# A graph transformer layer on one core: the search for edge windows by columns, the order of early loads, and the engine that computes two factors

## The chip, the cores and the metric

The kernel runs on one core of a Trainium2 chip (trn2). The metric is the device time of one execution in microseconds (us); given is the median of three runs. In the profile the engines are called PE (TensorE, matrix products; PEld is its weight load), DVE (VectorE), ACT (ScalarE), POOL (GpSimd) and SP (SyncE, which only issues transfers). Each engine takes its instructions in the order in which they were built, and waits at an instruction until the semaphores that it names are reached.

## The reference, cut to what matters

3125 nodes with 256 features, 53,125 edges sorted by their destination, float32. The layer normalizes x, adds a graph convolution and a linear attention with its own feed-forward part, and then a mixture of 16 experts.

```python
xn = _layernorm(x)
# graph part: weighted sum over the edges that end in a node, then a product
msgs = edge_weight[:, None] * xn[src]
agg = segment_sum(msgs, dst, 3125)
gnn = agg @ W.T + b
# mixer: linear attention over all nodes, 8 heads
Q, K, v = elu(xn @ Wq) + 1, elu(xn @ Wk) + 1, xn @ Wv / L
KV = einsum('nshd,nshv->nhdv', K, v)
...
msg = layernorm(attention @ Wm, g1, b1)
h = relu(concatenate([xn, msg]) @ W1) @ W2
mix = xn + layernorm(h, g2, b2)
x = x + gnn + mix
# experts: the best 2 of 16 for each node
x = x + moe(_layernorm(x))
```

## The kernel before

The nodes are laid out as 25 tiles (t) of 125 rows; a tile is 128 partitions by 256 features of `x_all`. All is in one program of one core; a scheduler of the framework orders instructions on each engine, and `tc.issue_after(instruction)` tells it behind which instruction some work is to stand.

The first stage goes over the 25 tiles. `moments` takes mean and variance of a batch of tiles (BATCHES gives the batches: tiles 0-1, 2-4, 5-9, 10-14, 15-19, 20-24) with bn_stats and bn_aggr, and the reciprocal root with a chain of small DVE instructions (`rsqrt`, L81 to L88). It also makes two factors, `by` (L347) and `less` (L348, L349). `normed(t)` makes the normalized tile `xn` on DVE (L361), transposes it on PE (L371), copies it to `xnT` on ACT (L372), and then rewrites the tile of `x_all` as x * by + less on ACT (L374) and adds the constant row `cb` on POOL (L375): this is x + xn plus two biases, the sum to which later parts are added. `projected(t)` multiplies the tile by the weights of the graph part, of the keys and of the values (L383, L385), makes `k_sb` from the keys (ACT L387 and L389, DVE L391), `v_sb` from the values with a column of ones (L393, L394), and `y_all` (L395), which is also stored in DRAM as `y_d` (L396). `summed` adds keys by values to `pkv` (L402), one tile behind.

Beside this stage runs `windows`, a generator whose pieces are put between the tiles (`pieces`; `normed` takes the next piece at tiles 1, 5, 6, 11, 12 and 13, and what is left is taken ahead of tile 16). It finds where the edges of each group of five nodes begin. There are 625 groups, kept as 125 partitions by GC = 5 columns. The destinations lie as 125 rows of 425 (`dst_sb`). The heads of the rows are compared with each group's first node (`cmp_h`, L214 to L219); POOL fetches that row for each group with an indirect DMA, one for each column (`rows`, L223); all columns are compared at once (`cmp_r`, L229, 125x2125), summed (L231), turned into a start (L232 to L235, `start_i`) and stored (L236); then POOL fetches a window of 128 edges for each group (`win`, L240, five indirect DMAs). From the windows come keys and weights (L246 to L285), which `adjacency` turns into blocks of the adjacency matrix: two wide DVE instructions (`one` L295, `wone` L300), 12 matmuls (L315), an ACT copy (L318), a store to DRAM (L319). There are 157 of these in a list `todo`; one is made per tile from tile 16 on, the others between the pieces of the mixer groups. A loop behind the stage (L440) would mend windows that are too short; its count, `loops`, is computed.

Then come seven mixer groups (L597: tiles, adjacencies and early messages of each group), the last messages with the gating, and the experts.

Loads: SP issues x of tiles 0-1, then `dst_sb`, then x of tiles 2-4 and 5-9, then Wq, Wm, W1, W2 and the constant rows behind `out` (L176), then the stores `y_d` as they come. ACT issues the three projection weights (`wcat`) and x of tiles 10-24 ahead of its first compute instruction. POOL issues small constants. A transfer's issue can wait for an older transfer that used the same semaphore.

Of the kernel before, what the change touches and what calls it, by code (L numbers as in the profile page):

```python
# [8 lines left out]
F32 = mybir.dt.float32  # L9
BF16 = mybir.dt.bfloat16  # L10
I32 = mybir.dt.int32
AF = mybir.ActivationFunctionType
ALU = mybir.AluOpType
AX = mybir.AxisListType
# [3 lines left out]
N = 3125  # L18
C = 256
E = 53125  # L20
P = 128
V = 125
# [4 lines left out]
F = 512  # L27
LANES = 128
# [12 lines left out]
EJ = E // V  # L41
GN = 5
NG = N // GN
GC = NG // V
WIN = 128
# [4 lines left out]
BATCHES = ((0, 2), (2, 5), (5, 10), (10, 15), (15, 20), (20, 25))  # L50
# [4 lines left out]
def tile_gps_layer(ctx: ExitStack, tc: tile.TileContext, a: dict, out: bass.AP):  # L55
    nc = tc.nc
# [12 lines left out]
    def row_bcast(src, n, name, pool=const):  # L69
        t = pool.tile([P, n], F32, name=name)  # L70
        nc.gpsimd.dma_start(t, bass.AP(tensor=src.tensor, offset=src.offset, ap=[[0, P], [1, n]]))
        return t
# [67 lines left out]
    first = ExitStack()  # L140
    w_first = first.enter_context(tc.tile_pool(name="w_first", bufs=1))
    dst_sb = w_mix.tile([V, EJ], I32, name="dst_sb")
    b2 = row_bcast(a["b2"], C, "b2", w_mix)
    gnn_b = row_bcast(a["gnn_b"], C, "gnn_b", w_mix)

    def load_x(queue, t0, t1):
        queue.dma_start(x_all[:, t0:t1, :], a["x"][:, t0:t1, :])

    wcat = w_mix.tile([128, 2, 3 * C], F32, name="wcat")
    load_x(nc.sync, *BATCHES[0])  # L150
    nc.sync.dma_start(dst_sb, a["dst"].rearrange("(p j) -> p j", p=V))
    for i, name in enumerate(("gnn_WT", "Wk", "Wv")):
        nc.scalar.dma_start(wcat[:, :, i * C : (i + 1) * C], a[name].rearrange("(k p) o -> p k o", p=128))

    for batch in BATCHES[1:3]:
        load_x(nc.sync, *batch)
    for batch in BATCHES[3:]:
        load_x(nc.scalar, *batch)
    wq = w_mix.tile([128, 2, C], F32, name="wq")
    nc.sync.dma_start(wq, a["Wq"].rearrange("(k p) o -> p k o", p=128))  # L160
    wm = w_mix.tile([128, 2, C], F32, name="wm")
    nc.sync.dma_start(wm, a["Wm"].rearrange("(k p) o -> p k o", p=128))
    w1 = w_mix.tile([128, 4, F], F32, name="w1")
    nc.sync.dma_start(w1, a["W1"].rearrange("(k p) o -> p k o", p=128))
    w2 = w_mix.tile([128, 4, C], F32, name="w2")
    nc.sync.dma_start(w2, a["W2"].rearrange("(k p) o -> p k o", p=128))
    g1 = const.tile([128, 2], F32, name="g1")
    nc.gpsimd.dma_start(g1, a["g1"])
    b1 = const.tile([128, 2], F32, name="b1")
# [2 lines left out]
    gate_b = row_bcast(a["gate_b"], NE, "gate_b")  # L172
    gate_w = const.tile([128, 2, NE], F32, name="gate_w")
    nc.gpsimd.dma_start(gate_w, a["gate_w"].rearrange("(k p) e -> p k e", p=128))

    nc.sync.dma_start(out[N:, :].rearrange("(p r) (k c) -> p (r k) c", r=2, k=2),  # L176
                      ones[:, None, :].to_broadcast([LANES, 4, P]))
    cb = w_mix.tile([P, C], F32, name="cb")
    nc.gpsimd.tensor_tensor(cb, b2, gnn_b, op=ALU.add)

# [18 lines left out]
    def windows():  # L199
# [13 lines left out]
        shape = [V, GC, V]  # L213
# [9 lines left out]
            nc.gpsimd.indirect_dma_start(out=rows[:, i, :], out_offset=None, in_=dst_v,  # L223
                                         in_offset=bass.IndirectOffsetOnAxis(ap=row_i[:, i : i + 1], axis=0))
        yield
        cmp_r = prep.tile([V, GC, EJ], BF16, name="cmp_r")
        start_f = prep.tile([V, GC], F32, name="start_f")
        shape = [V, GC, EJ]
        nc.vector.tensor_tensor(cmp_r, rows, thr[:, :, None].to_broadcast(shape), op=ALU.is_lt)  # L229
        yield  # L230
        nc.vector.tensor_reduce(start_f, cmp_r, AX.X, ALU.add)  # L231
        nc.vector.scalar_tensor_tensor(start_f, row_f, float(EJ), start_f, op0=ALU.mult, op1=ALU.add)  # L232
        nc.vector.tensor_scalar(start_f, start_f, float(E - WIN), None, op0=ALU.min)
        start_i = prep.tile([V, GC], I32, name="start_i")
        nc.vector.tensor_copy(start_i, start_f)  # L235
        nc.sync.dma_start(first_d.rearrange("(i r) o -> r (i o)", r=V), start_i)  # L236

        win = prep.tile([V, GC, WIN, 3], I32, name="win")
        for i in range(GC):
            nc.gpsimd.indirect_dma_start(out=win[:, i, :, :].rearrange("p e w -> p (e w)"), out_offset=None,  # L240
                                         in_=a["edges"][:, :],
                                         in_offset=bass.IndirectOffsetOnAxis(ap=start_i[:, i : i + 1], axis=0))
        yield
        shape = [V, GC, WIN]
        src_f = prep.tile(shape, F32, name="src_f")
# [92 lines left out]
    mv = w_mix.tile([P, NT, 2], F32, name="mv")  # L338
    by = w_mix.tile([P, NT], F32, name="by")
    less = w_mix.tile([P, NT], F32, name="less")  # L340
    ready = {}

    def moments(t0, t1):
        for i in range(t0, t1):
            stats(mv[:, i, :], x_all[:, i, :])
        ready[t0] = rsqrt(mv[:, t0:t1, 1], t1 - t0)
        nc.gpsimd.tensor_scalar(by[:, t0:t1], ready[t0], 1.0, None, op0=ALU.add)  # L347
        nc.gpsimd.tensor_tensor(less[:, t0:t1], mv[:, t0:t1, 0], ready[t0], op=ALU.mult)  # L348
        nc.gpsimd.tensor_scalar(less[:, t0:t1], less[:, t0:t1], -1.0, None, op0=ALU.mult)  # L349

    pieces = windows()
    with tc.issue_after(next(pieces).ins):
# [1 line left out]
    def normed(t):  # L354

        nonlocal rstd, r0
        for t0, t1 in BATCHES:
            if t == t0:
                rstd, r0 = ready.pop(t0), t0
        xn = work.tile([P, C], F32, name="xn", bufs=4)  # L360
        ins = nc.vector.tensor_scalar(xn, x_all[:, t, :], mv[:, t, 0:1], rstd[:, t - r0 : t - r0 + 1],  # L361
                                      op0=ALU.subtract, op1=ALU.mult)
        with tc.issue_after(ins.ins):
            if t in (1, 5, 6, 11, 12, 13):
                next(pieces, None)
            for b in range(len(BATCHES) - 1):
                if t == BATCHES[b][0] + 1:
                    moments(*BATCHES[b + 1])
        ptr = a_ps.tile([128, 2, P], F32, name="tok", bufs=3)
        for k in range(2):  # L370
            nc.tensor.transpose(ptr[:, k, :], xn[:, k * 128 : (k + 1) * 128], ident)  # L371
        nc.scalar.copy(xnT[:, :, t * P : (t + 1) * P], ptr)  # L372

        nc.scalar.activation(x_all[:, t, :], x_all[:, t, :], AF.Identity, scale=by[:, t : t + 1], bias=less[:, t : t + 1])  # L374
        nc.gpsimd.tensor_tensor(x_all[:, t, :], x_all[:, t, :], cb, op=ALU.add)  # L375

    def projected(t):

        cols = slice(t * P, (t + 1) * P)
        pyk = a_ps.tile([P, 2 * C], F32, name="big")  # L380
        pv = a_ps.tile([P, C], F32, name="tok", bufs=3)
        for k in range(2):
            nc.tensor.matmul(pyk, lhsT=xnT[:, k, cols], rhs=wcat[:, k, : 2 * C], start=(k == 0), stop=(k == 1))  # L383
        for k in range(2):
            last = nc.tensor.matmul(pv, lhsT=xnT[:, k, cols], rhs=wcat[:, k, 2 * C :], start=(k == 0), stop=(k == 1))  # L385
        ek = work.tile([P, C], F32, name="ek", bufs=2)
        nc.scalar.activation(ek, pyk[:, C:], AF.Exp)  # L387
        k_sb = work.tile([P, C], F32, name="k_sb")
        nc.scalar.activation(k_sb, pyk[:, C:], AF.Relu)  # L389

        nc.vector.scalar_tensor_tensor(k_sb, ek, 1.0, k_sb, op0=ALU.min, op1=ALU.add)  # L391
        v_sb = work.tile([P, 2, 129], F32, name="v_sb")
        nc.vector.memset(v_sb[:, :, 128:129], 1.0)  # L393
        nc.scalar.activation(v_sb[:, :, :128], pv.rearrange("p (c v) -> p c v", c=2), AF.Copy, scale=1.0 / N)  # L394
        nc.scalar.copy(y_all[:, t, :], pyk[:, :C])  # L395
        nc.sync.dma_start(y_d[t * P : (t + 1) * P, :], y_all[:, t, :])  # L396
        return last, k_sb, v_sb

    def summed(t, k_sb, v_sb):
# [6 lines left out]
    kept = None  # L406
    normed(0)
    for t in range(NT):
        if t == 16:
            for _ in pieces:  # L410
                pass
            prep_pool.close()
            nbr = first.enter_context(tc.tile_pool(name="nbr", bufs=3))
            half = ExitStack()
            hot = half.enter_context(tc.tile_pool(name="hot", bufs=3))
        if t + 1 < NT:
            normed(t + 1)
        if t >= 16:
            adjacencies(1)
        last, *taken_on = projected(t)  # L420

        if kept is not None:
            with tc.issue_after(last.ins):
                summed(t - 1, *kept)
        kept = taken_on
# [168 lines left out]
            nc.vector.scalar_tensor_tensor(xt, hw[:, i, :], rstd[:, i : i + 1], xt, op0=ALU.mult, op1=ALU.add)  # L594

    t = 0
    for nt, n_adj, n_early in ((4, 16, 0), (4, 22, 6), (4, 22, 7), (4, 22, 7), (3, 22, 6), (3, 22, 7), (3, 22, 2)):  # L597

        pieces = 3 * nt + 6
        i = 0  # L600
        for p, _ in enumerate(mixer(t, nt)):
            while i < n_adj and i * pieces < (p + 1) * n_adj:
                adjacencies(1)
                i += 1
                if i * n_early // n_adj > (i - 1) * n_early // n_adj:
                    messages(*early.pop(0))
        adjacencies(n_adj - i)
        t += nt
# [554 lines left out]
```

## Time and profile before

| what | value |
|---|---|
| median of 3 runs | 1083.58 us |
| lowest, highest | 1080.57, 1085.25 us |
| the profiled execution | 1079.18 us |
| its span | 1077.5 us |
| mean granted clock of PE in it | 0.991 |
| ACT busy share, POOL busy share | 25%, 20% |
| PE busy in the stretch 20 to 40 us, 40 to 60 us | 14.52, 13.15 us |
| DVE in these | 14.33, 11.58 us |
| share of the 16 DMA engines in 0 to 20, 20 to 40, 40 to 60 us | 0.92, 0.57, 0.39 |

An engine's busy share is the time in which it has an instruction under way. The page's slices cut the span into 40 equal parts, with a digit for the tenths of each that were busy; the row PEclk gives the clock that PE was granted. A wait is named by the instruction that stood waiting, and by what released it.

### The profile page before, as it was taken

What the parts mean: (1) busy time and instruction counts of PE and PEld (TensorE: products, weight loads), DVE (VectorE), ACT (ScalarE), POOL (GpSimd) and SP (SyncE); (2) the same over time, 40 slices, a digit from 0 to 9 for tenths busy, and PEclk for the clock granted to TensorE, in tenths of its full rate; (3) what the DMA queues carried; (4) which work ended last, traced back from release to release, by engine and by line L of the source; (5) the groups of instructions that cost most, each with busy time, mean ns of one, the idle gap of its engine ahead of it and who ended that gap; (6) DMA issues with size and microseconds to landing.
All of it is one profiled execution on the core that took longest, in us unless ns stands there. A gap on an engine that the chain in (4) does not pass through costs nothing.

```text
span 1077.5 us, 16415 instructions
## 1 busy us (share of the span) xinstructions
PE 1022.2 (95%) x6074; PEld 824.2 (76%) x6074; DVE 612.2 (57%) x1741; ACT 266.9 (25%) x582; POOL 215.0 (20%) x211
## 2 busy tenths in 40 slices
PE   4699989999999999999999999989999999999995
PEld 2467666778678787878878888878788888888884
DVE  5697695859579497976981135565942222222221
ACT  2456442333323333232320000103111111111110
POOL 6642000000000000000000001012454544454432
PEclk9899999999999999999999999999999999999998
DMA  9402241324234243444434454574665767576762
GB/s 279 99 25 85 103 170 66 118 88 166 100 131 163 89 144 141 157 157 156 167 101 156 158 174 139 179 260 154 186 174 162 239 201 233 168 230 183 225 194 27
DMA packets 70754, 165.66 MB, mean 154 GB/s; under 512 B 10966, under 2 KB 30318, under 8 KB 66698
## 3 DMA queue, kind: packets, MB, share of 16 engines
q1 hardware_dynamic: 50264, 133.14, 35.8%
q0 software_dynamic: 15904, 25.43, 10.8%
q10 hardware_dynamic: 4498, 5.95, 1.6%
q8 instruction: 50, 0.82, 0.3%
q14 instruction: 38, 0.31, 0.1%
HBM read 106.06 MB, written 58.40 MB: 153 GB/s over the span
## 4 chain that ended last, share of the span: by engine, by line
PE 64%; DVE 19%; DMA 3%; issue 1%; POOL 0%; ACT 0%; DVEq 0%; POOLq 0%; ACTq 0%
PE ph L891 18%; PE po L916 9%; PE pb L506 8%; PE po L635 7%; PE big L576 7%; DVE wone L300 6%; PE pa L506 4%; DVE one L295 4%; PE pa L315 3%; PE tok L585 3%; DMA nbr<-adj_d 1%; PE tok L554 1%; DVE bn_st L93 1%; PE ptr L877 1%; DMA xb<-xn_d,from_e 1%
## 5 line engine op out<-in xcount | busy, mean ns | idle before, releaser
L891 PE MATMUL ph<-xTb,wt 128*128 128x256 f32 (+1 forms) x992 | 214.8, 365 | 0.7 <-ACT xTb L880 0.7
L891 PEld LDWEIGHTS ph<-xTb,wt 128*128 128x128 f32 x992 | 175.7, 190 | 28.0 <-ACT xTb L880 7.3
L300 DVE TENSOR_TENSOR wone<-one,wgts 128x1536 bf16<-128x1536 bf16 x150 | 142.2, 953 | 28.4 <-PE pa L315 28.3
L506 PE MATMUL pb<-y_all,nbr 128*128 128x256 f32 x608 | 146.9, 383 | 0.8 <-DMA nbr<-adj_d 0.8
L315 PEld LDWEIGHTS <-one 128*128 128x128 bf16 x1875 | 119.9, 97 | 31.9 <-issue 14.3
L315 PE MATMUL pa<-wone,one 128*128 128x128 bf16 x1875 | 135.0, 218 | 5.5 <-DVE wone L300 2.7
L318 ACT COPY adj<-pa 128x512 f32<-128x512 f32 (+1 forms) x157 | 91.0, 586 | 149.7 <-PE pa L315 124.9
L898 DVE TENSOR_TENSOR hid<-hid,ph 128x512 f32<-128x512 f32 (+1 forms) x62 | 40.0, 645 | 150.9 <-PE ph L891 150.8
L506 PEld LDWEIGHTS pb<-y_all,nbr 128*128 128x128 f32 x608 | 109.7, 190 | 14.7 <-DMA nbr<-adj_d 1.0
L916 PE MATMUL po<-wt,hid 128*128 128x256 f32 x456 | 113.5, 381 | 0.6 <-DVE yb L919 0.6
L635 PE MATMUL po<-y_all,nbr 128*128 128x256 f32 x450 | 104.2, 385 | 4.5 <-DVE at_u L815 3.4
L295 DVE TENSOR_TENSOR one<-iota,keys 128x1024 bf16<-128x1024 bf16 x150 | 102.2, 698 | 2.1 <-POOL wgts L277 2.1
L635 PEld LDWEIGHTS po<-y_all,nbr 128*128 128x128 f32 x450 | 84.2, 192 | 16.2 <-DVE at_u L815 3.8
L920 POOL DMA_INDIRECT out<-yb,to_l x45 | 71.5, 1589 | 117.9 <-DVE yb L919 66.4
L648 POOL IOTA rev<- 125x16 f32 x1 | 0.2, 155 | 460.9 <-DVE rs_v L81 460.9
L916 PEld LDWEIGHTS po<-wt,hid 128*128 128x128 f32 x456 | 82.2, 190 | 12.9 <-DVE yb L919 1.4
L897 ACT ACTIVATE hid<-ph 128x512 f32<-128x512 f32 (+1 forms) x62 | 34.9, 563 | 208.3 <-PE ph L891 208.3
L919 DVE TENSOR_SCALAR yb<-po,sh 128x256 f32<-128x256 f32 x57 | 27.6, 484 | 57.9 <-PE po L916 55.5
L383 PE MATMUL big<-wcat,xnT 128*128 128x512 f32 x100 | 51.2, 635 | 0.0
L576 PE MATMUL big<-xnT,w 128*128 128x512 f32 (+1 forms) x112 | 49.6, 555 | 0.0
L508 DVE TENSOR_TENSOR x_all<-x_all,pb 128x512 f32<-128x512 f32 (+1 forms) x33 | 21.7, 657 | 48.8 <-PE pb L506 48.6
L689 ACT COPY xT<-ph 128x256 f32<-128x256 f32 x25 | 8.7, 373 | 162.4 <-PE ph L687 119.7
(268 smaller groups left out, 1249.3 us busy)
## 6 DMA issues: line engine op xcount, KB each, us to landing
wt<-in_w SPq DMA_DIRECT2D x28, 1536.0 KB, 8.1
adj_d<-adj SPq DMA_DIRECT2D x156, 256.0 KB, 2.2
nbr<-adj_d SPq DMA_DIRECT2D x25, 576.0 KB, 4.3
nbr<-adj_d SPq DMA_DIRECT2D x50, 256.0 KB, 2.6
nbr<-adj_d SPq DMA_DIRECT2D x25, 512.0 KB, 3.3
wt<-in_w POOLq DMA_DIRECT2D x3, 1536.0 KB, 11.8
y_d<-y_all SPq DMA_DIRECT2D x25, 128.0 KB, 1.7
out<-x_all ACTq DMA_DIRECT2D x25, 125.0 KB
```

The lines of the kernel that those rows point to most:

```text
L295: nc.vector.tensor_tensor(one.rearrange("p b h e j -> p (b h) e j"), iota_2[:, None, :, :].to_broadcast(shape), ql.rearrange("p b h j -> p ...
L300: nc.vector.tensor_tensor(wone, one[:, :, 1:2, :, :].to_broadcast(shape), w[:, :, :, None, :].to_broadcast(shape), op=ALU.mult)
L315: nc.tensor.matmul(pa[:, j, :], lhsT=one[:, j // 2, 0, :, j % 2], rhs=wone[:, j // 2, i, :, j % 2], start=(i == 0), stop=(i == 2))
L318: nc.scalar.copy(rows[:, :n, :], pa[:, :n, :])
L383: nc.tensor.matmul(pyk, lhsT=xnT[:, k, cols], rhs=wcat[:, k, : 2 * C], start=(k == 0), stop=(k == 1))
L506: nc.tensor.matmul(pb[:, i, :], lhsT=rows[:, k - t0, :], rhs=y_all[:, k, :], start=(k == t0 and i == 0), stop=(k == t1 - 1), skip_group_ch ...
L576: nc.tensor.matmul(ph[:, :w], lhsT=w1[:, k, j * 128 : (j + 1) * 128], rhs=rhs, start=(k == 0), stop=(k == 3))
L635: last = nc.tensor.matmul(pg, lhsT=rows[:, k - t0, :], rhs=y_all[:, k, :], start=(k == t0), stop=(k == t1 - 1))
L891: last = nc.tensor.matmul(p[:, m, :w], lhsT=self.wt[:, i, k * F + at : k * F + at + 128], rhs=self.xT[:, k, :w], start=(k == 0), stop=(k = ...
L898: self.units = nc.vector.tensor_tensor(hid, hid, pre[1], op=ALU.mult)
L916: last = nc.tensor.matmul(po[:, r, :], lhsT=self.hid[:, k, r * LANES : (r + 1) * LANES], rhs=self.wt[:, 2, k * C : (k + 1) * C], start=(k ...
L920: made.append(nc.gpsimd.indirect_dma_start(out=out[:, :], out_offset=bass.IndirectOffsetOnAxis(ap=at, axis=0), in_=yb[:, r, :], in_offset= ...
```

## The change

Four things change.

1. `windows` finds the starts column by column: for each of the five columns a comparison of 425 elements, its sum, the three small instructions of the start and the column's window gather, with a yield between columns; the store of the starts comes behind the last. The pieces are taken at other tiles (one at 1, 4, 9, 10 and 11, two at 5 and 6), and the rest ahead of tile 14, where adjacencies now begin; the first mixer group makes 14 of them where it made 16.
2. `by` and `less` are made on VectorE, in two instructions instead of three on GpSimd.
3. The ACT rewrite of `x_all` and the POOL addition move from `normed` to `projected`, behind the copy that makes `v_sb`. `v_sb` is a ring of three tiles made once, with its columns of ones set once, in the place of a memset per tile.
4. `dst_sb` is loaded first, ahead of x of tiles 0-1. x of tiles 10-24, Wq, Wm, W1, W2 and the constant rows of `out` are issued by SP, each behind the `y_d` store of an early tile.

```diff
+    nc.sync.dma_start(dst_sb, a["dst"].rearrange("(p j) -> p j", p=V))
...
-    load_x(nc.sync, *BATCHES[0])
-    nc.sync.dma_start(dst_sb, a["dst"].rearrange("(p j) -> p j", p=V))
+    load_x(*BATCHES[0])
...
-    for batch in BATCHES[3:]:
-        load_x(nc.scalar, *batch)
...
+    def load_later(t):
+
+        if t in (0, 1, 3):
+            load_x(*BATCHES[{0: 3, 1: 4, 3: 5}[t]])
+        if t in (5, 6, 7, 8):
+            w, name = ((wq, "Wq"), (wm, "Wm"), (w1, "W1"), (w2, "W2"))[t - 5]
+            nc.sync.dma_start(w, a[name].rearrange("(k p) o -> p k o", p=128))
+        if t == 9:
+            nc.sync.dma_start(out[N:, :].rearrange("(p r) (k c) -> p (r k) c", r=2, k=2),
+                              ones[:, None, :].to_broadcast([LANES, 4, P]))
...
-        cmp_r = prep.tile([V, GC, EJ], BF16, name="cmp_r")
...
-        nc.vector.tensor_tensor(cmp_r, rows, thr[:, :, None].to_broadcast(shape), op=ALU.is_lt)
-        yield
-        nc.vector.tensor_reduce(start_f, cmp_r, AX.X, ALU.add)
...
         for i in range(GC):
+            at = slice(i, i + 1)
+            cmp_r = prep.tile([V, EJ], BF16, name="cmp_r", bufs=2)
+            nc.vector.tensor_tensor(cmp_r, rows[:, i, :], thr[:, at].to_broadcast([V, EJ]), op=ALU.is_lt)
+            nc.vector.tensor_reduce(start_f[:, at], cmp_r, AX.X, ALU.add)
+            nc.vector.scalar_tensor_tensor(start_f[:, at], row_f[:, at], float(EJ), start_f[:, at], op0=ALU.mult,
+                                           op1=ALU.add)
+            nc.vector.tensor_scalar(start_f[:, at], start_f[:, at], float(E - WIN), None, op0=ALU.min)
+            nc.vector.tensor_copy(start_i[:, at], start_f[:, at])
             nc.gpsimd.indirect_dma_start(out=win[:, i, :, :].rearrange("p e w -> p (e w)"), out_offset=None,
...
+            if i < GC - 1:
+                yield
...
-        nc.gpsimd.tensor_scalar(by[:, t0:t1], ready[t0], 1.0, None, op0=ALU.add)
-        nc.gpsimd.tensor_tensor(less[:, t0:t1], mv[:, t0:t1, 0], ready[t0], op=ALU.mult)
-        nc.gpsimd.tensor_scalar(less[:, t0:t1], less[:, t0:t1], -1.0, None, op0=ALU.mult)
+        nc.vector.tensor_scalar(by[:, t0:t1], ready[t0], 1.0, None, op0=ALU.add)
+        nc.vector.scalar_tensor_tensor(less[:, t0:t1], mv[:, t0:t1, 0], -1.0, ready[t0], op0=ALU.mult, op1=ALU.mult)
...
-            if t in (1, 5, 6, 11, 12, 13):
+            for _ in range({1: 1, 4: 1, 5: 2, 6: 2, 9: 1, 10: 1, 11: 1}.get(t, 0)):
                 next(pieces, None)
...
-        v_sb = work.tile([P, 2, 129], F32, name="v_sb")
-        nc.vector.memset(v_sb[:, :, 128:129], 1.0)
+        v_sb = v_ring[t % 3]
...
+        stored = nc.sync.dma_start(y_d[t * P : (t + 1) * P, :], y_all[:, t, :])
+        with tc.issue_after(stored.ins):
+            load_later(t)
+        with tc.issue_after(v_copy.ins):
+            nc.scalar.activation(x_all[:, t, :], x_all[:, t, :], AF.Identity, scale=by[:, t : t + 1],
+                                 bias=less[:, t : t + 1])
+        nc.gpsimd.tensor_tensor(x_all[:, t, :], x_all[:, t, :], cb, op=ALU.add)
...
-        if t == 16:
+        if t == 14:
...
-        if t >= 16:
+        if t >= 14:
             adjacencies(1)
...
-    for nt, n_adj, n_early in ((4, 16, 0), (4, 22, 6), (4, 22, 7), (4, 22, 7), (3, 22, 6), (3, 22, 7), (3, 22, 2)):
+    for nt, n_adj, n_early in ((4, 14, 0), (4, 22, 6), (4, 22, 7), (4, 22, 7), (3, 22, 6), (3, 22, 7), (3, 22, 2)):
```

In the changed program the rewrite of `x_all` on ACT is L406, the addition on POOL L408, the memsets of the ring L349, the factors L356 and L357, a column's comparison L237.

## The prediction

> **What bounds the kernel now.** First the page: how much of the span TensorE (PE) works, and where it doesn't.
>
> ```profile
> span 1077.5 us, 16415 instructions
> PE 1022.2 (95%) x6074; PEld 824.2 (76%) x6074; DVE 612.2 (57%) x1741; ACT 266.9 (25%) x582; POOL 215.0 (20%) x211
> PE   4699989999999999999999999989999999999995
> DVE  5697695859579497976981135565942222222221
> PEclk9899999999999999999999999999999999999998
> ```
>
> PE is the bound: 1022.2 of 1077.5 us. So an edit is worth the PE idle time (and half-clock time) that it removes, 55 us in all. Next, the waits of PE between 0 and 130 us (us in all, times, longest):
>
> ```profile
> PE pkv L402 <- DVE v_sb L393: 9.7, 2, 6.9
> PE pa L209 <- DVE heads L207: 8.3, 1, 8.3
> PE tok L371 <- DVE xn L361: 2.9, 1, 2.9
> PE pkv L402 <- DVE start_f L232: 2.6, 1, 2.6
> ```
>
> Once the projections have begun (12 us), three waits stand out: 2.85 (9.7 less 6.85), 2.63 and 6.85 us. The engine named is where they end; the cause is one step back. The timeline tells it (start, duration, instruction, idle before it):
>
> ```profile
> 24.60 0.60 ACT L374 ACTIVATE x_all<-x_all,less,by 128x256 f32<-128x256 f32 x1 [4.67 <-POOL less L349]
> ...
> 31.62 2.37 DVE L229 TENSOR_TENSOR cmp_r<-rows,thr 125x2125 bf16<-125x2125 int32 x1 [1.08 <-DMA rows<-in_dst,row_i]
> ...
> 34.65 2.36 DVE L231 TENSOR_REDUCE start_f<-cmp_r 125x5 f32<-125x2125 bf16 x1
> ...
> 45.09 1.21 POOL L240 DMA_INDIRECT win<-in_edges,start_i  x1 [0.31 <-issue]
> ...
> 52.13 0.58 DVE L246 CAST src_f<-win 125x640 f32<-125x640 int32 x1 [8.12 <-DMA win<-in_edges,start_i]
> ...
> 54.32 1.20 PE L402 MATMUL pkv<-v_sb,k_sb 125*128 125x129 f32 x4 [6.85 <-DVE v_sb L393]
> ```
>
> Wait 1 (PE idle 23.6 to 26.4): ACT stood 4.67 us before L374, because `less` sat on POOL behind five row gathers (15.75 to 23.2). Wait 2 (34.85 to 37.48): 4.7 us of cmp_r and its reduction stood on DVE ahead of `k_sb`. Wait 3 (47.47 to 54.32): DVE stood at L246 until the last window, issued at 45.09, had landed, with `k_sb` of tile 6 queued behind. After waits 1 and 3 the granted clock falls (stretch: its length, busy times of PE, PEld, DVE, ACT, POOL; then clock, DMA share, GB/s), and further on DVE takes over:
>
> ```profile
> 26.00:28.00 2.00, 1.57 (x7) 1.60 (x8) 1.87 (x8) 2.00 (x8) 1.15 (x3) 0.64 0.83 231
> 28.00:30.00 2.00, 2.00 (x3) 0.76 (x3) 1.73 (x10) 0.36 (x2) 0.29 (x2) 0.51 0.72 242
> ...
> 54.00:56.00 2.00, 1.68 (x7) 1.71 (x8) 2.00 (x8) 0.02 (x1) 0.00 (x0) 0.50 0.00 0
> ...
> 155.00:160.00 5.00, 2.60 (x34) 1.95 (x31) 5.00 (x14) 1.76 (x3) 0.00 (x0) 1.00 0.66 232
> ```
>
> Clock lost after wait 1: 1.57 x 0.36 + 2.00 x 0.49 = 1.55 us. After wait 3 the clock is 0.50 at 54 to 56 and 0.68 at 56 to 58, some 1.5 us. The last row is the first mixer group: DVE full, PE half. Last, the gathers from issue to landing, rows and then win:
>
> ```profile
> DMA to landing us min/median/max: 9.4/10.2/10.4
> DMA to landing us min/median/max: 7.0/8.8/10.1
> ```
>
> **The change part by part.** I follow the order of the built program, queue by queue, laid end to end with the durations of the trace. On DVE a small instruction takes 0.10 us, or 0.20 behind one that it waits for (rows of rsqrt at 9.06 to 9.54); xn and bn_stats occupy 0.37, k_sb 0.34. A tile of projection takes PE 3.25 us when nothing stops it (59.75, 63.00, 66.25). The same laying of the old program ends the projections at 124.4, where the trace ends them at 123.6, so I trust the method to about 1 us.
>
> *Start.* dst goes ahead of x[0:2] on SP. The second transfer there landed at 7.6 before (L206), and the two hold the same bytes together, so x[0:2] lands at about 7.6. bn_stats stood at 8.07 behind d0 and heads, which now run earlier: 0.45 gained. `by` and `less` stand ahead of the first xn: 0.35 lost. I take 0; x[0:2] 1.5 us later or earlier moves all by about that.
>
> *Factors on VectorE (wait 1).* POOL loses 18 small instructions, DVE gains 12 and loses 22 memsets of 0.06 us: even in sum. ACT puts L374 behind the v copy and reaches it with `less` ready; its six instructions for a tile take 1.85 us of 3.25, so it hides. Wait 1 and its clock loss go: 2.85 + 1.55. Next late is column 0 of cmp_r, which the program places on DVE right behind xn of tile 4, ahead of k_sb of tile 2 and xn of tile 5. Gather 0 is issued at 15.75 as before. Landing in the new traffic is unknown: 2.6 us (a 256 KB nbr load, page part 6) to 10.4. Four MB of loads no longer run beside it, which is more like the windows' case (7.0 to 8.8), so I take 8: 23.8. Behind it stand comparison 0.50 and reduction 0.49 (a fifth of 2.4; at most the 0.70 of L295, five times wider), 20 small ones 2.5 us, k_sb 0.34: xn of tile 5 starts at 27.6 and PE, free at 27.05, goes on at 28.1. New wait 1.0; none below a landing of 7, 3.4 us at 10.4.
>
> *Columns (wait 2).* 25 instructions instead of 5. Between xn of tile 6 (30.5) and of tile 7 stand xn 0.37, two comparisons and reductions 2.0, 12 small 1.2, k_sb 0.34, five bn_stats 1.85, four aggregations 0.4: 36.5. PE is free at 34.55 and goes on at 36.9: a wait of 2.35 for 2.63. Gained 0.3, for the batch's bn_stats take the place of the wide instructions.
>
> *Windows (wait 3).* Column 4 has its start at 35.4; POOL issues window gathers 3 and 4 at 35.6 and 37.1 (1.5 us apart as before), against 43.56 and 45.09. The adds L408 that stand between the gathers on POOL have their input by then. Landing: 2.6 to 10.1 again; I take 7.0, the row of the last one (45.09 to 52.1), since the other gathers are spread and go 1.5 to 11 us ahead: 44.1. DVE stands there with src_f ahead of k_sb of tile 6: then 2.5 us of src_f, src_a, src_r and rsqrt, and k_sb at 46.6. PE has done tile 7's projection at 42.95 (36.9 + 2 x 3.25 - 0.45) and goes on at 47.05. Wait 4.1 for 6.85; the half clock after it stays. The same matmul started at 54.32: **7.25 us gained up to here**.
>
> *Earlier adjacencies.* Tiles 14 and 15 now carry one adjacency each: a tile with one takes 3.99 us (107.82, 111.81): 2 x 0.74 = 1.5 lost. The waits of 0.35 and 1.46 us at L269, for ACT's `turned` copies, shrink to 0.9, as four L374 no longer crowd ahead of them: 0.9 gained. Projections end 6.65 us earlier.
>
> *First mixer group, 14 adjacencies for 16.* From 127.8 to 164.9 the chain of waits is DVE; an adjacency holds 0.86 (wone) + 0.60 (one) of it. 2 x 1.46 = 2.9 gained. PE idles 5.3 us between 128 and 170, so it doesn't take over at once; should it, only 1.5 is gained.
>
> *Loads behind stores.* x[10:15] moves from ACT's queue to SP behind the y_d store of tile 0: issued at 18.0, wanted by bn_stats at 32.9. That leaves 14.9 us, and the x load that shows a landing took 12.6 in full traffic: cover of 2.3, each us beyond it stops DVE by as much. x[15:20] (20.9) and x[20:25] (27.4) are wanted over 20 us later; Wq, Wm, W1, W2 by about 52 us are wanted at 117. The filler rows of out wait for nobody. A load delays the next store's issue by 0.4 us; only the repair loop reads y_d. 0.
>
> *Two rules weighed.* The trace halves the clock after 2.85 us idle and not after 2.63. The Trainium skill ("TensorE: Matmul & The Clock Gate", Part 1: The HAM clock gate) puts the drop at an idle window of about 3.4 us; by it wait 1 would have cost no clock and the sum would be 1.55 smaller, 8.0; the trace decides. Against the columns speaks "Perfetto Trace Analysis", Optimizing Scalar/DVE Operations: some 60 ns of overhead for each DVE instruction, so group them; 20 more would cost 1.2 us by it. By the rows I have 20 x 0.10 = 2.0, already in the steps above, so by the page the sum would be up to 0.8 larger.
>
> **Sum**: 6.65 + 2.9 = 9.6 us (9.55). On the profiled execution 1079.18 becomes 1069.6. That execution lies 4.4 under the median of the runs, 1083.58, so I forecast 1083.58 - 9.6 = **1074.0**. Bounds: all gathers at 2.6 us remove the waits of 1.0 and 4.1 and the second clock loss (some 2.0), less 1.3 of small waits elsewhere: 5.8 better, 1068.2. Gathers at 10.4 and 10.1: 2.4 + 3.1 = 5.5 worse, and with the mixer's 1.5 instead of 2.9: 1080.9.
>
> **Rivals.** About 0.5% (5.4 us) is what a measurement tells from no change.
>
> *The wait stays (0.19).* Gathers keep 10 us and DVE, which waits in order, passes it all on: about 1079 to 1081. For it: rows took 9.4 to 10.4, and windows up to 10.1 in light traffic. Against it: the last window took 7.0.
>
> *The gathers get fast (0.12).* With the loads gone they land like an nbr load: 1068 to 1069. For it: DMA share 1.0 at 14 to 24 us before. Against it: windows took 7 us at a share near 0.6.
>
> *The circle (0.09), slower.* POOL's gathers 3 and 4 stand behind the add L408 of tile 4, which needs ACT, which needs PE, which needs k_sb from DVE, which stands at src_f for those gathers' predecessors. If each delay feeds the next, the last window lands late, 1 us for 1 us. It eats the gain at a landing of 44.1 + 9.6 = 53.7 and is slower by over 0.5% from 59, 22 us after the issue now laid at 37.1; at 60 the time is 1090. Against it: the adds need only tile 4, which PE finishes at 31.
>
> That the columns don't come early is excluded by the built order. My forecast's own case, 1069.5 to 1078.2, has 0.60. Faster by over 0.5%: 0.60 + 0.12 = 0.72; within: 0.19; slower: 0.09. Range 1067 to 1081: the bounds above, 1 us wider at the fast end.
>
> **What would show it.** No wait of ACT for `less`; a DVE wait of about 1.4 us for rows near 23 and of 5 to 6 us for win near 40; PE idle near 27 (1.0), 36 (2.4) and 45 (4.1); one stretch of half clock, not two, past 20 us; projections ending near 117; PE less idle at 140 to 160. I am wrong if the last window is issued after 40 us, x[10:15] stops DVE, or the first xn comes after 13 us.

## The result, and the profile after

The changed kernel took 1084.78 us (median of 22 executions, 1079.2 to 1093.0), the kernel before 1083.59 beside it (22 executions). The ratio is 1.0001, 95% interval 0.9981 to 1.0021: no change that can be measured, where 1074.0 was forecast. The profiled execution took 1085.7 us. Its page:

```profile
span 1084.1 us, 16411 instructions
PE 1026.4 (95%) x6074; PEld 826.9 (76%) x6074; DVE 617.2 (57%) x1751; ACT 267.4 (25%) x582; POOL 206.6 (19%) x193
PE   6589999999999999999999999989899999999995
PEclk9899999999999999999999999999999999999998
```

PE works as long as before; the idle time has not gone. The waits of PE from 0 to 130 us (us in all, times, longest):

```profile
PE pkv L414 <- DVE rs_y L88: 7.6, 1, 7.6
PE pa L213 <- DVE heads L211: 7.2, 1, 7.2
PE tok L379 <- DVE xn L369: 5.2, 2, 3.4
PE pkv L414 <- DVE k_sb L396: 2.7, 1, 2.7
PE tok L379 <- DVE mv L94: 2.1, 1, 2.1
```

The 7.2, and 3.4 of the 5.2, are the start; 1.82 of the 5.2 is the new first wait. The wait for the windows is 7.55 where it was 6.85, and a wait of 2.7 is new. The timeline of the changed kernel at the places where the prediction had its steps (start, duration, instruction, idle before it):

```profile
21.36 0.57 DVE L237 TENSOR_TENSOR cmp_r<-rows,thr 125x425 bf16<-125x425 int32 x1
...
22.48 1.33 DVE L82 TENSOR_SCALAR rs_h<-rs_v 128x5 f32<-128x5 f32 x1
...
23.04 1.43 POOL L408 TENSOR_TENSOR x_all<-x_all,cb 128x256 f32<-128x256 f32 x2
...
28.78 0.41 PE L379 MATMUL tok<-ident,xn 128*128 128x128 f32 x2 [1.82 <-DVE xn L369]
...
35.87 0.29 SPq L248 DMA_DIRECT2D first_d<-start_i  x1
...
37.63 1.24 POOL L243 DMA_INDIRECT win<-in_edges,start_i  x1 [0.31 <-DVE mv L94]
...
48.30 0.59 DVE L252 CAST src_f<-win 125x640 f32<-125x640 int32 x1 [8.29 <-DMA win<-in_edges,start_i]
...
51.36 1.20 PE L414 MATMUL pkv<-v_sb,k_sb 125*128 125x129 f32 x4 [7.55 <-DVE rs_y L88]
```

Column 0 finds its rows landed and does not wait. The last window gather is issued at 37.63 instead of 45.09, as laid out, but lands 10.7 us later instead of 7.0. Stretches of the same kernel (length, busy PE, PEld, DVE, ACT, POOL, then clock, DMA share, GB/s):

```profile
38.00:40.00 2.00, 2.00 (x7) 0.99 (x7) 1.97 (x6) 0.64 (x2) 1.76 (x2) 1.00 1.15 76
40.00:42.00 2.00, 2.00 (x12) 1.47 (x11) 0.01 (x1) 1.73 (x6) 0.46 (x1) 1.00 0.91 94
...
50.00:52.00 2.00, 0.64 (x3) 0.67 (x4) 2.00 (x8) 0.00 (x0) 0.00 (x0) 0.50 0.18 69
52.00:54.00 2.00, 2.00 (x7) 1.46 (x7) 2.00 (x7) 0.37 (x1) 0.00 (x0) 0.50 0.03 8
54.00:56.00 2.00, 2.00 (x3) 0.67 (x2) 2.00 (x6) 0.00 (x0) 0.00 (x0) 0.50 0.00 0
56.00:58.00 2.00, 2.00 (x9) 1.57 (x8) 2.00 (x5) 1.13 (x4) 0.00 (x0) 0.68 0.00 0
```

At 38 to 42 the DMA engines are full and move 76 to 94 GB/s; packets stand there rather than run. Behind the long wait PE works at half clock from 51.36 to past 56. Points of the two profiled executions, from DVE's timeline (us; gained is before less after):

| point | before | after | gained | predicted |
|---|---|---|---|---|
| first xn | 11.51 | 10.88 | 0.6 | 0 |
| xn of tile 7 | 39.86 | 36.64 | 3.2 | 3.4 |
| PE goes on after the windows | 54.32 | 51.36 | 3.0 | 7.25 |
| first kvz copy (projections ended) | 123.59 | 124.27 | -0.7 | 6.65 |
| first eq of mixer group 0 | 127.81 | 130.53 | -2.7 | 6.65 |
| first eq of group 1 | 187.78 | 190.48 | -2.7 | 9.55 |
| first eq of group 2 | 245.83 | 246.20 | -0.4 | 9.55 |
| first eq of group 6 (the last) | 508.02 | 508.35 | -0.3 | 9.55 |

Behind 508 us the two run the same program, and there the executions differ by themselves: from that point to the end the 14 profiled executions of this study took 569.4 to 580.7 us, in no order of their versions. So a version is best read at 508 and by the ratio of many executions. Even at 508 one execution tells differences only down to about 1 us: a variant of the kernel before whose edit moved nothing (experiment 2) stands at 509.19 there, 1.2 us later. Unless a ratio is given, the numbers below are of one profiled execution each.

### The profile page after: what moved, and what is told of

Same layout as the page of the kernel before. It is cut to its first block, busy times and chain, and to the rows that moved or that the text cites. A ratio compares the mean times of both kernels' runs of the same rounds, so it can differ in the third digit from the quotient of the medians.

```text
span 1084.1 us, 16411 instructions
## 1 busy us (share of the span) xinstructions
PE 1026.4 (95%) x6074; PEld 826.9 (76%) x6074; DVE 617.2 (57%) x1751; ACT 267.4 (25%) x582; POOL 206.6 (19%) x193
## 3 DMA queue, kind: packets, MB, share of 16 engines
q1 hardware_dynamic: 50696, 135.11, 36.5%
## 4 chain that ended last, share of the span: by engine, by line
PE 64%; DVE 19%; DMA 3%; issue 1%; POOL 0%; ACT 0%; DVEq 0%; POOLq 0%; ACTq 0%
PE ph L903 18%; PE po L928 9%; PE pb L518 8%; PE po L647 7%; PE big L588 7%; DVE wone L306 6%; PE pa L518 4%; DVE one L301 4%; PE pa L321 3%; PE tok L597 3%; DMA nbr<-adj_d 2%; PE tok L566 1%; PE ptr L889 1%; DMA xb<-xn_d,from_e 1%; DVE bn_st L93 1%
## 5 line engine op out<-in xcount | busy, mean ns | idle before, releaser
L301 DVE TENSOR_TENSOR one<-iota,keys 128x1024 bf16<-128x1024 bf16 x150 | 99.5, 678 | 0.0
```

Source lines behind the costliest of these rows:

```text
L301: nc.vector.tensor_tensor(one.rearrange("p b h e j -> p (b h) e j"), iota_2[:, None, :, :].to_broadcast(shape), ql.rearrange("p b h j -> p ...
```

## The experiments

**1. The store of the starts, the weights, POOL's adds.** In the packet records of the changed kernel, 4608-byte packets of the window gathers take 178 ns in the median until 38 us and none over 0.97 us (the text of the expectation, 178 to 250 ns, is too narrow: 23 of 120 took longer). Of those that begin between 38 and 45 us nine take over 1 us (longest 5031 ns), and 1024-byte packets of another queue up to 3959 ns. What begins just before is the store to `first_d`: 625 packets of 4 bytes, 36 to 39 us.

```diff
-        nc.sync.dma_start(first_d.rearrange("(i r) o -> r (i o)", r=V), start_i)
...
+        if t == 20:
+            nc.sync.dma_start(first_d.rearrange("(i r) o -> r (i o)", r=V), start_i)
```

> The changed kernel with one edit: the store of the starts to first_d (625 pieces of 4 bytes, issued at 35.9 us, seen on the queues from 36 to 39) goes out behind the y_d store of tile 20. Theory S, the small pieces hold the DMA engines up: 4608-byte packets took 178 to 250 ns before 38 us and up to 5.0 ms/1000 (5031 ns) after; without the store they stay near 0.2 us, the last window gather (issued 37.6) lands in 4 to 5 us instead of 10.6, and the PE wait of 7.55 us that ends at 51.4 falls to 2 to 3.5 us; the span falls by 4 to 6 us, less what later waits take back. Theory W, the weights moved behind the stores share the engines with the gathers: the store is nothing, landing 10 us and the wait 7 to 8 us stay, the time stays within 0.2%. Theory G, such gathers take 7 to 10 us whatever runs beside them: as W.

The wait is 2.57, the projections end at 118.98 (124.27) and group 6 starts at 503.07 (508.35). Ratio to before 0.9979 (0.9953 to 1.0005). Stretches of this kernel, and then its timeline:

```profile
38.00:40.00 2.00, 2.00 (x8) 1.21 (x7) 1.75 (x4) 0.65 (x4) 1.72 (x2) 1.00 0.71 179
40.00:42.00 2.00, 2.00 (x10) 1.26 (x10) 0.00 (x0) 1.38 (x5) 0.73 (x1) 1.00 0.49 171
```

```profile
42.40 0.63 DVE L254 CAST src_f<-win 125x640 f32<-125x640 int32 x1 [2.62 <-DMA win<-in_edges,start_i]
...
46.03 0.68 PE L416 MATMUL pkv<-v_sb,k_sb 125*128 125x129 f32 x4 [2.57 <-DVE rs_y L88]
```

About twice the GB/s at little more than half the share, no 4608-byte packet over 0.70 us from 38 us on, and the last gather (issued 37.72) landed 4.7 us later. Theory S holds here.

```diff
-        if t in (5, 6, 7, 8):
+        if t in (14, 15, 16, 17):
...
-        if t == 9:
+        if t == 18:
```

> The changed kernel with one edit: Wq, Wm, W1, W2 and the filler rows go out behind the y_d stores of tiles 14 to 18 instead of 5 to 9, so that no weight load is issued before the last window gather has landed. Theory W: the last gather lands in 6 to 7 us instead of 10.6, the PE wait of 7.55 us falls to about 4, the span falls by 3 to 4 us. Theory S (the 4-byte store at 36 us): the gathers still stall from 38 us, landing 8 to 10 us, the wait stays between 6 and 8 us and the time within 0.2%. Theory G: landing and wait unchanged.

PE's wait for the windows in this kernel:

```profile
49.39 1.20 PE L414 MATMUL pkv<-v_sb,k_sb 125*128 125x129 f32 x4 [5.54 <-DVE rs_y L88]
```

Wait 5.54, the last gather lands in 8.7 us, group 6 at 507.36, ratio 1.0018 (0.9990 to 1.0045). The packets stall as before (10 over 1 us, longest 4489 ns). The weights cost 2 us of this wait while the store holds the engines up; theory W explains that part and no more.

```diff
-        nc.gpsimd.tensor_tensor(x_all[:, t, :], x_all[:, t, :], cb, op=ALU.add)
```

> The changed kernel without the 25 adds of cb to x_all on POOL (L408), so its output lacks that constant. Theory P, POOL's tensor operations slow the small VectorE instructions that run beside them (0.65 to 1.33 us instead of 0.16 between 23 and 28 us): the rsqrt instructions of batch 2 come back to 0.16, xn of tile 5 starts near 26 instead of 28.24 and its PE wait of 1.8 us goes; xn of tile 7 starts near 34.5 instead of 36.64. The rival, that VectorE waits for ACT or for DMA there: durations stay above 0.6 and xn of tiles 5 and 7 stay within 0.3 us. Wait 3 is set by the gathers and moves only as far as they are issued earlier (about 2 us).

One instruction of the rsqrt ahead of xn of tile 5, in this kernel:

```profile
24.57 0.16 DVE L82 TENSOR_SCALAR rs_h<-rs_v 128x5 f32<-128x5 f32 x1
```

L82 took 1.33 us in the changed kernel. Without the adds the small instructions of that rsqrt all take 0.16 to 0.17 us; xn of tile 5 comes at 27.21 (28.24), xn of tile 7 at 35.28 (36.64), and the wait of 1.82 is gone. Theory P holds, for 1.0 to 1.4 us here. (This kernel leaves out the constant, so its output lacks it.)

**2. The store in the kernel before.** The same edit of the store, in the kernel before:

```diff
-        nc.sync.dma_start(first_d.rearrange("(i r) o -> r (i o)", r=V), start_i)
...
+        if t == 20:
+            nc.sync.dma_start(first_d.rearrange("(i r) o -> r (i o)", r=V), start_i)
```

> The kernel before with the one edit of the first kernel of this set: the store to first_d goes out behind the y_d store of tile 20. No weight load runs beside the window gathers here (38.9 to 52.1 us), so theory W gives no change: landing 7 to 10 us, PE wait 6.85 us. Theory G: no change either. Theory S: 4608-byte packets stay near 0.2 us instead of a mean of 0.48 and a maximum of 4.3, the last gather (issued 45.1) lands in 4 to 5 us instead of 7.0, and the PE wait falls from 6.85 to about 4; the span falls by 2.5 to 3 us, 0.25%.

No gain (wait 7.7, ratio 0.9999, 0.9973 to 1.0025), and the reason was not the one in the expectation: without a tie the scheduler had issued the store as soon as its input was ready, at 39 us, so the run says nothing about any theory. With the tie:

```diff
+        stored = nc.sync.dma_start(y_d[t * P : (t + 1) * P, :], y_all[:, t, :])
+        if t == 20:
+            with tc.issue_after(stored.ins):
+                nc.sync.dma_start(first_d.rearrange("(i r) o -> r (i o)", r=V), start_i)
```

> The kernel before with the store of the starts tied behind the y_d store of tile 20 (in the earlier try of this the built program kept the store in its old place, at 39 us, so that run told nothing). Theory S, the 625 pieces of 4 bytes hold up whatever is on the DMA engines: 4608-byte packets stay near 0.2 us on the mean instead of 0.48, the last window gather lands in 4 to 5 us instead of 7.0, the PE wait falls from 6.85 to 3.5 to 4.5 us and the last mixer group starts 2.5 to 3 us earlier than 508.0. Theory G, gathers of 4608 bytes that start on idle DMA engines are slow in themselves: wait 6.5 to 7.7 us, packets of 1 to 4 us remain.

With the store behind tile 20, DVE's and PE's wait for the windows:

```profile
49.44 0.72 DVE L246 CAST src_f<-win 125x640 f32<-125x640 int32 x1 [4.43 <-DMA win<-in_edges,start_i]
...
51.98 0.68 PE L405 MATMUL pkv<-v_sb,k_sb 125*128 125x129 f32 x4 [3.23 <-DVE v_sb L393]
```

The last gather lands in 4.5 us instead of 7.0, the wait is 3.23 instead of 6.85; of 200 packets none takes over 0.81 us, where 23 took over 1 us. Theory G falls: the kernel before was held up by its own store, and the 7.0 on which the prediction built was already a stalled landing. The projections end 2.4 us earlier, but group 6 starts only 0.9 earlier. The likely reason is the clock behind the loop: it was 0.66 at 125 to 130 us in this execution and 1.00 in that of before, some 1.7 us of PE's work. Ratio 0.9981 (0.9952 to 1.0010).

**3. Number of pieces.** The store at its place, in another layout:

```diff
-        nc.sync.dma_start(first_d.rearrange("(i r) o -> r (i o)", r=V), start_i)
+        nc.sync.dma_start(first_d.rearrange("(r i) o -> r (i o)", r=V), start_i)
```

> The changed kernel with the store of the starts at its place (35.9 us) but row by row: 125 pieces of 20 bytes instead of 625 of 4 (the repair loop looks them up by the other order). Theory S as a matter of the number of pieces: the stall shrinks to a fifth, some 1.5 us, the last gather lands in 5 to 6 us and the PE wait is 3 to 4 us instead of 7.55. If it is each small write to DRAM, whatever their number down to 125, that holds the queues: the wait stays at 6 us or more.

DVE's and PE's wait for the windows in this kernel:

```profile
42.84 0.62 DVE L252 CAST src_f<-win 125x640 f32<-125x640 int32 x1 [3.10 <-DMA win<-in_edges,start_i]
...
46.42 0.68 PE L414 MATMUL pkv<-v_sb,k_sb 125*128 125x129 f32 x4 [1.20 <-DVE rs_y L88]
```

The 125 pieces of 20 bytes run from 36.3 to 38.0 us. The wait is 1.20, the last gather lands in 5.5 us, group 6 starts at 505.28. So in fewer pieces the store can stay at its place. Number and size of the pieces change together here; which of the two counts was not tried.

**4. Adjacencies.**

```diff
-        if t == 14:
+        if t == 16:
...
-    for nt, n_adj, n_early in ((4, 14, 0), ...
+    for nt, n_adj, n_early in ((4, 16, 0), ...
```

> The changed kernel with the adjacencies back at tile 16 and 16 of them in the first mixer group. By the built program VectorE has 20 adjacencies ahead of the first mixer group's mw in both versions, so theory F (the planner fills the first group from the next one) expects the stretch from the first eq of group 0 to that of group 1 unchanged at 59.9 to 60.0 us, and the one from group 1 to group 2 2.3 to 2.4 us longer than the 55.7 of the changed kernel. The projections end 1.5 us earlier (two adjacencies of 0.74 us less), or up to 4 us earlier if the PE wait of 2.7 us at 75 goes too. The prediction's own reading: the first group's stretch is 2.9 us longer with 16 than with 14.

From the first eq of group 0 to that of group 1: 59.95 us with 16 and with 14. From group 1 to group 2: 58.05 with 16, 55.72 with 14. The projections end at 123.23, 1.0 earlier. Theory F holds: between the projections and the first group's mw DVE makes 20 adjacencies in either program, since the built order fills up from the next group. The two fewer pay 2.3 us, one group later.

**5. POOL beside VectorE, and the four together.** In the changed kernel the split of `wgts` on POOL now falls on the rsqrt of tiles 15 to 19:

```profile
66.77 1.69 POOL L285 TENSOR_TENSOR turned<-turned,wgts 128x650 f32<-128x650 f32 x1
66.95 1.53 DVE L86 TENSOR_TENSOR rs_s<-rs_y 128x5 f32<-128x5 f32 x1
...
74.81 0.38 DVE L396 SCALAR_TENSOR_TENSOR k_sb<-ek,k_sb 128x256 f32<-128x256 f32 x1
...
75.34 0.69 PE L414 MATMUL pkv<-v_sb,k_sb 125*128 125x129 f32 x4 [2.66 <-DVE k_sb L396]
```

```diff
-            nc.gpsimd.tensor_copy(part, pairs[:, 2])
+            nc.vector.tensor_copy(part, pairs[:, 2])
...
-                nc.gpsimd.tensor_tensor(pairs[:, 2], pairs[:, 2], part, op=ALU.subtract)
+                nc.vector.tensor_tensor(pairs[:, 2], pairs[:, 2], part, op=ALU.subtract)
```

> The changed kernel with the store of the starts late (as in the first experiment) and the five instructions that split wgts (L283 and L285, 0.75 to 1.7 us each on POOL) on VectorE. Theory P, POOL's tensor operations stretch VectorE's small ones: the rsqrt of batch 5 goes back to 0.16 us an instruction from 0.6 to 1.4, the PE wait for k_sb near 66 to 75 us falls from 3.1 us to below 1.5 although VectorE has 3 to 4 us more to do, and the projections end 1.5 to 2.5 us earlier than the 118.9 of that experiment. The rival, that VectorE simply has too much to do there: the wait stays at 3 us or grows to 5, and the projections end at 119 to 121.

The same matmul in this kernel:

```profile
67.60 0.68 PE L416 MATMUL pkv<-v_sb,k_sb 125*128 125x129 f32 x4 [0.72 <-DVE k_sb L398]
```

0.72 instead of 3.1 (2.66 in the changed kernel), though DVE does five instructions of 0.82 us more; the projections end at 117.34, 1.6 earlier than with the late store alone. Theory P holds for the wait; the last experiment, with the same edits, also has 0.7 there, but its projections end at 118.24, so the 1.6 is known to about 1 us.

```diff
+        held.append(t)
+        if t >= 15:
+            for _ in range(min(3, len(held))):
+                u = held.pop(0)
+                with tc.issue_after(v_copy.ins):
+                    nc.gpsimd.tensor_tensor(x_all[:, u, :], x_all[:, u, :], cb, op=ALU.add)
```

> The changed kernel with four edits: the store of the starts late, the weights behind the stores of tiles 14 to 18, the split of wgts on VectorE, and the adds of cb held back to tiles 15 to 24. If theories S and P both hold, xn of tile 7 starts near 35.3 instead of 36.6, the PE wait for the windows is 1 to 2.5 us, the waits for xn and k_sb shrink to 1 us each, the projections end at 114.5 to 117, and the last mixer group starts 7 to 9 us before the 508.0 of the kernel before: ratio 0.991 to 0.994. If POOL's adds were no cost, the projections end at 117 to 119 and the ratio is 0.995 to 0.997.

A miss: projections end at 120.51, group 6 starts at 504.82, ratio 0.9973 (0.9950 to 0.9995). In this execution column 0 had to wait for its rows (first line of the next fence), and all that follows came 2.5 us later. Whether that is chance or belongs to the held-back adds was not tried. It is not all: 2.5 us less would be 118.0, still outside the 114.5 to 117 expected, and the ratio, of 12 executions, misses 0.991 to 0.994. So no gain of the weights and of the held-back adds beside the other two edits is shown.

**6. The other parts undone.** First the loads as before, then the factors and the rewrite of `x_all` as before, each in the changed kernel.

```diff
+    for t0, t1 in BATCHES[3:]:
+        nc.scalar.dma_start(x_all[:, t0:t1, :], a["x"][:, t0:t1, :])
...
+    for w, name in ((wq, "Wq"), (wm, "Wm"), (w1, "W1"), (w2, "W2")):
+        nc.sync.dma_start(w, a[name].rearrange("(k p) o -> p k o", p=128))
...
     def load_later(t):
+        return
```

```diff
-        nc.vector.tensor_scalar(by[:, t0:t1], ready[t0], 1.0, None, op0=ALU.add)
+        nc.gpsimd.tensor_scalar(by[:, t0:t1], ready[t0], 1.0, None, op0=ALU.add)
+        nc.gpsimd.tensor_tensor(less[:, t0:t1], mv[:, t0:t1, 0], ready[t0], op=ALU.mult)
+        nc.gpsimd.tensor_scalar(less[:, t0:t1], less[:, t0:t1], -1.0, None, op0=ALU.mult)
```

> The changed kernel with the loads issued as in the kernel before: x[10:25] on ACT's queue at the start, the four weights and the filler rows on SP's at the start. Theory: this part of the change buys the rows gathers their early landing (5.3 us for the first, and column 0 compared at 21.36 without a wait, against 9.4 and more before). With the loads back, the first column waits for its rows until 24 to 26 us, PE waits 1 to 4 us for xn of tile 5, the window gathers are issued 2 to 4 us later than 37.6, and the projections end 2 to 4 us later than 124.2. The rival, that the order of loads is nothing: all within 0.7 us.

> The changed kernel with by and less on POOL and the rewrite of x_all right behind the copy of xnT, as before. The prediction took 2.85 us of PE wait and 1.55 us of clock from this part. If so, the wait near 26 to 29 us is 2.5 to 4 us and the clock of the stretch 20 to 40 falls from 1.00 to about 0.91; xn of tile 7 starts 3 to 5 us later than 36.6. The rival, that the wait is now set by the columns on VectorE and the rows: xn of tile 7 moves by less than 1 us. VectorE's part of the loop body is 114 instructions here, so theory J has little or no stall (0 to 1.5 us) at the loop.

Lines of three timelines: the first is of the kernel with the four edits (all_four), the second of the one with the old loads, the third of the one with the old factors:

```profile
25.28 0.78 DVE L240 TENSOR_TENSOR cmp_r<-rows,thr 125x425 bf16<-125x425 int32 x1 [2.47 <-DMA rows<-in_dst,row_i]
```

```profile
27.44 0.61 DVE L245 TENSOR_TENSOR cmp_r<-rows,thr 125x425 bf16<-125x425 int32 x1 [3.77 <-DMA rows<-in_dst,row_i]
```

```profile
24.55 0.60 ACT L383 ACTIVATE x_all<-x_all,less,by 128x256 f32<-128x256 f32 x1 [4.87 <-POOL less L358]
```

With the old loads DVE stands for the rows and compares column 0 6.1 us later than in the changed kernel (27.44 for 21.36), PE waits 2.67 for xn of tile 5, and the projections end at 127.97, 3.7 later. With the old factors ACT stands again for `less`, PE waits 3.0 at 26.4, the clock of 20 to 40 us is 0.83, xn of tile 7 comes 2.3 us later (less than the 3 to 5 expected), the window gathers run into a longer stall (PE wait 9.5) and the projections end at 130.63, 6.4 later. So both parts gain: the loads 3.7 us; the factors 2.3 at tile 7, and 6.4 at the end of the projections, of which the longer stall is a part. The columns and the ring of `v_sb` were not undone by themselves.

**7. The jump over the repair loop.** Between the first and second half of the kvz copies DVE jumps over the body of a loop that makes no pass here. DVE's next copy behind it, in the kernel before, the changed kernel, and the last experiment:

```profile
126.73 0.18 DVE L431 COPY kvz<-pkv 32x32 f32<-32x32 f32 x1 [2.06 <-issue]
```

```profile
129.44 0.18 DVE L443 COPY kvz<-pkv 32x32 f32<-32x32 f32 x1 [4.10 <-PE pa L321]
```

```profile
121.36 0.18 DVE L445 COPY kvz<-pkv 32x32 f32<-32x32 f32 x1 [2.05 <-issue]
```

PE is not the cause, whatever the releaser says: the copy waits for no semaphore. In the event records 13 instructions of the loop's exit (12 waits and a branch) follow each other at 0.1 us, but in the changed kernel DVE stands 2.13 us between the third and the fourth, and the semaphores that the fourth names were last raised at 125.24, 3 us before it ran. How long it stood, and where, goes with the number of DVE instructions in the body that is jumped over, as counted in the built programs:

| body of the loop, DVE instructions | stood, us | where |
|---|---|---|
| 107 (no_cb), 112 (before) | none | |
| 114 (factors_old) | 1.56 | behind 9 exit waits |
| 120 (changed kernel and four others) | 2.11 to 2.15 | behind 3 |
| 124 (store_rows), 132 (wgts_vector, all_four) | 2.3 to 2.5 | ahead of the first |

The body grew from 112 to 120 with the change, by waits that the framework put into it. The last experiment adds this to wgts_vector:

```diff
-            nc.vector.tensor_scalar(p_s, p_s, -1000.0, None, op0=ALU.add)
+            nc.gpsimd.tensor_scalar(p_s, p_s, -1000.0, None, op0=ALU.add)
```

> The changed kernel with the store of the starts late, the split of wgts on VectorE, and, in the repair loop, which runs no pass on this input, the 25 steps of p_s by -1000 on POOL: VectorE's part of the loop body shrinks from 132 to 83 instructions. Theory J, the jump over the body costs VectorE an instruction fetch when the body is long: between the branch and the copies of kvz behind it VectorE stood for 2.1 us with a body of 120 (changed kernel), 2.5 with 132, and not at all with 107 and 112 (before). With 83 it does not stand: the exit waits follow each other at 0.1 us, kvz first to last copy takes 4.0 to 4.6 us instead of 6.5, the last mixer group starts 2 us earlier than the 502.65 of the kernel with the long body, and the ratio to before is 0.993 to 0.996. The rival, that the stall comes from where the code happens to lie: it stays at 2.1 to 2.5 us.

No stall with a body of 83; first to last kvz copy 4.04 us, group 6 at 500.23. The ratio is 0.9876 (0.9838 to 0.9914), median 1073.62 (6 executions) against 1086.52 in the same set: better than both kernels. The kernel before took 1082.5 to 1083.9 in the other sets, so part of the difference may belong to this set. Its window wait is 2.53. By the point at 508 it gains 7.8 us, by the executions 9 to 18; the rest lies in the stretch behind 508 and is not explained.

## Why the prediction was wrong, point by point

- *Start*: 0 predicted, 0.6 gained.
- *Factors on VectorE (wait 1)*: right. Wait 1 went and the clock of 20 to 40 us is 1.00 (0.91 before); undone, ACT stands 4.87 us for `less` again. The new wait was put at 1.0 and is 1.82, and its cause was taken wrongly: rows landing at 23.8, where column 0 ran at 21.36 without waiting. POOL's adds, moved later, stretched the rsqrt beside them (no_cb).
- *Two rules weighed*: the 1.55 us of clock came out, the rule behind it did not. The trace of before keeps 1.00 after 2.63 us of waiting (38 to 40 us); the same matmul in the kernel of experiment 2 with the tie waits 2.58 and the clock of 38 to 40 us is 0.50; with the late store (experiment 1) a wait of 3.09 at 70 us leaves it at 1.00. The length of a wait alone does not decide.
- *Columns (wait 2)*: right, 2.09 for 2.35, and xn of tile 7 at 36.64 for 36.5 (the step's own terms add up to 36.66). In part this is luck: column 0 came 2.4 us earlier than laid, and the stretched rsqrt took most of it back.
- *Windows (wait 3)*: **the first step that failed.** "Landing: 2.6 to 10.1 again; I take 7.0, the row of the last one (45.09 to 52.1), since the other gathers are spread and go 1.5 to 11 us ahead." It was 10.7. The gathers did go ahead, but the store of the starts went just as far ahead, and its 625 packets met them again: undone, 4.7 us in the changed kernel and 4.5 in the one before. The prediction named every queue past which the loads moved, but priced the store nowhere. This took 4.3 of the 7.25 us. "The half clock after it stays" failed with it: PE went on at 51.36 instead of 54.32, but the half clock lasted past 56 us in both kernels, so it cost 3.0 us (0.64 x 0.5 + 4.00 x 0.5 + 2.00 x 0.32) instead of 1.5.
- *Loads behind stores* at 0: wrong in both directions. Undone they cost 3.7 us at the end of the projections, since the rows land earlier without them; and placed where they are, the weights take 2 us of wait 3 for as long as the store stalls (one execution each).
- *Earlier adjacencies*: two adjacencies cost about what was said, and the two waits for `turned` (1.81 in all) went altogether where 0.9 was forecast; but the wait of 2.66 at 75 us was not seen: the split of `wgts` on POOL, now 10 us earlier, lies beside the rsqrt of tiles 15 to 19. The step gave POOL's instructions no price.
- *The stage's end*: a jump that cost 2.0 us more than before (127.81 - 123.59 = 4.22 against 6.26) was in no step.
- *First mixer group*: the place was wrong, the size nearly right: 0 there, 2.3 in the group behind it, for 2.9. Both programs have 20 adjacencies between the projections and mw; they were not counted.
- *Bounds*: the fast one takes off 2.0 us for the second half clock, for which the text works out 1.5. It does not bear on the outcome.

At 508 us, 9.55 predicted became -0.3. Of these 9.9, four terms make 9.6: 4.3 (windows), 2.7 (k_sb), 2.0 (jump) and 0.6 (mixer). That they come so close is in part luck: the 1.5 of half clock and the 0.9 of `turned` stand beside them and nearly cancel. None of the signs of being wrong that the prediction names came (the last window was issued at 37.63, the first xn at 10.88, DVE did not stop for x[10:15]); what failed was not among them. Of the rivals *the wait stays* came nearest: the landing was its 10 us. Its time of 1079 to 1081 still holds the mixer's gain in full and knows neither the wait for k_sb nor the jump.

On DVE beside POOL the rows come first: L86 took 1.53 us beside a POOL operation of 1.69, and 0.15 in the kernel with the split on VectorE. The Trainium skill ("SBUF — State Buffer", SBUF: two separate sides) says that a port pair is shared by the two as an exclusive lock, that whichever instruction starts first keeps it to its end, and that on VectorE's side instructions with two SBUF inputs are among those that need it, against a GpSimd operation that reads SBUF. L86 and L87 have two, and the POOL operation reads `turned`; the runs agree, and L86 ends at 68.48 where the POOL operation ends at 68.46. L82 and L83 have one input and were stretched as well (1.33 and 0.98), which those two inputs do not explain.

## What to carry to other kernels

Count the packets of every transfer that an edit moves, not only its bytes and who waits for it: 2.4 KB in 625 pieces held up gathers and other transfers for some 6 us; in 125 pieces the last gather landed in 5.5 us instead of 10.7. An engine that is idle is not free to use: a wide GpSimd operation beside a chain of small VectorE instructions made some of them four to nine times longer (0.65 to 1.53 us instead of 0.16), and putting it on VectorE itself was the cheaper place here. Where a scheduler orders the work, read the built order for each edit, and compare versions at a point ahead of the stage that varies by itself.

## What the runs showed of the hardware that was not expected

- 625 writes of 4 bytes to DRAM, each some 9 ns in its own record, let packets of other queues stand for up to 5.0 us (the long ones began at 38 to 45 us, the writes ran from 36 to 39); 125 writes of 20 bytes in 1.7 us let a packet stand for at most 1.5.
- A jump over 114 or more instructions cost DVE 1.6 to 2.5 us, none at 112 or fewer; where it stood fits a reach of some 123 instructions past the jump (114 + 9, 120 + 3), but not that nothing was seen at 112. That this is the fetching of instructions is argued from packets of the instruction queues near it (8192 bytes at 126.62 in the changed kernel), not shown; the kernel before has such a packet too, at 125.95, and did not stop.
- Why the stretch behind 508 us varies by 11 us between executions stays open.
